# Attention scores, and the first v projection, computed in four 64x64 quarters of the TensorE array

## The chip, the cores and the metric

The kernel runs on one core of a Trainium2 chip. A core has a matrix engine (TensorE, PE in the profile, with its weight loads listed apart as PEld), a vector engine (VectorE, DVE), an activation engine (ScalarE, ACT), a general engine (GpSimd, POOL) and a queue that issues DMAs (SyncE, SP). TensorE writes its results to PSUM, eight banks of 512 fp32 columns on 128 partitions; the other engines work from SBUF or read PSUM. The metric is the device time of one execution in microseconds (us), smaller is better. Every time below comes from repeated runs of the kernel or from one execution taken by the hardware profiler.

## What is computed

The reference is one attention block on a picture of 48x48 = 2304 tokens with 512 channels, for 4 pictures:

```python
hn  = group_norm(x, 32 groups) * gn_scale + gn_bias
qkv = einsum('oc,bchw->bohw', qkv_w, hn) + qkv_b
q, k, v = qkv.reshape(b, 3, 8, 64, t).astype(float16)   # 8 heads of 64
w   = softmax(einsum('bhct,bhcs->bhts', q * scale, k * scale))
a   = einsum('bhts,bhcs->bhct', w, v).astype(float32)
out = x + einsum('oc,bchw->bohw', proj_w, a) + proj_b
```

Here b = 4, c = 512, t = 2304, and scale is 64 to the power of -1/4.

## The kernel before

**Tiling.** A batch's x lies in SBUF as 4 chunks of 128 channels by 5 token blocks (`QBLOCKS`: four of 512, one of 256). Heads are taken in pairs: a pair g (16 of them, 4 per batch) has one tile q and one tile k of 128 partitions, the even head in partitions 0 to 63 and the odd one in 64 to 127, by 2304 tokens, in fp16. The v values of two pairs lie in one tile with tokens on the partitions (18 tiles of 128 tokens, `NT`).

**Projections.** `qk_chain` (L709) makes a block of q or k: for each of 4 chunks, two fp32 matmuls with 64 weight columns each, one into PSUM partitions 0 to 63 and one into 64 to 127. `v_chain` (L760) makes v for two token tiles in one PSUM bank, again in two column halves: 2 tiles x 4 chunks x 2 halves = 16 matmuls of 256 columns; then one VectorE addition (L768) adds the bias and writes v. The trace shows each fp32 matmul as two records, one of each half starting together.

**Attention.** It runs over `stream`: for each pair and each query block a row of units, 27 per pair and so 432 in all. `scores` (L932) handles one unit: three PSUM tiles `ps` of two banks each. For each of them (a block of 512 queries) it multiplies 128 keys by 512 queries for both heads: two matmuls of 64 contraction rows and 128 weight columns, one per head, in the two row halves of the array, one per bank. In a block of 256 queries each `ps` tile takes two key tiles, so four matmuls of 256 columns. ScalarE then exponentiates the `ps` tile into p (L939). `values` (L957) multiplies p by v: 128 contraction rows, 64 weight columns per head, so two column halves. VectorE adds p over the units (L986); `add_up` (L1009) sums over the keys with a matmul against ones; `proj_chain` (L837) is the output projection, with the array undivided (128 weight columns, 128 rows).

**Order.** The program's order is written by hand. Before the attention (`alone` is true) the first pair's q and k and then batch 0's first v half are projected, with `ps` tiles as their banks (three `ps` tiles, two banks each). In the attention loop each step n issues the scores of unit n, VectorE's sum of unit n-1, pieces of projection work that a planner (`fill`) lets through against a credit, and the values of unit n-2. The planner's costs are constants in the code, so the order does not depend on measured time. TensorE works through its instructions in that order.

The lines that matter below: L709 (q and k projection), L760 and L768 (v projection and its evacuation), L932 and L939 (scores and exponential), L957 (values), L837 (output projection), L1009 (sums).

Of the kernel before, what the change touches and what calls it, by code (L numbers as in the profile page):

```python
# [12 lines left out]
F32 = mybir.dt.float32  # L13
F32R = mybir.dt.float32r
F16 = mybir.dt.float16
I32 = mybir.dt.int32
AF = mybir.ActivationFunctionType
ALU = mybir.AluOpType
# [4 lines left out]
B, C, T = 4, 512, 48 * 48  # L23
HEADS, D = 8, 64
GROUP = C // 32
EPS = 1e-5
P = 128
NC = C // P
NPAIR = HEADS // 2
NG = B * NPAIR  # L30
NT = T // P
# [11 lines left out]
QB = 512  # L43
# [424 lines left out]
def fast_path(  # L468
# [12 lines left out]
    nc = tc.nc  # L481
# [5 lines left out]
    vpool = ctx.enter_context(tc.tile_pool(name="vpool", bufs=1))  # L487
    apool = ctx.enter_context(tc.tile_pool(name="apool", bufs=2 * NPAIR - 1))
    ppool = ctx.enter_context(tc.tile_pool(name="ppool", bufs=3))
    work = ctx.enter_context(tc.tile_pool(name="work", bufs=2))  # L490
    small = ctx.enter_context(tc.tile_pool(name="small", bufs=2))
    dram = ctx.enter_context(tc.tile_pool(name="dram", bufs=4, space=DRAM))
    ps_s = ctx.enter_context(tc.tile_pool(name="ps_s", bufs=3, space=PSUM))
# [4 lines left out]
    hn = {}  # L498
# [24 lines left out]
    wqkv = const.tile([P, NC, 3 * C], F32, name="wqkv")  # L523
# [21 lines left out]
    bv = const.tile([P, C], F32, name="bv")  # L545
# [38 lines left out]
    def chain_bank(name):  # L584
        if alone[0]:
            return ps_s.tile([P, 2, QB], F32, tag="ps", name=name)[:, 0, :]
        return ps_w.tile([P, QB], F32, tag="pw", name=name)
# [88 lines left out]
    def chain_pieces(us, one, steps):  # L676


        def run(chunks):
            for c in chunks:  # L680
                one(c)

        return [
            piece(us * len(chunks), lambda chunks=chunks: run(chunks), i == 0, last)
            for i, chunks in enumerate(steps)
            for last in (i == len(steps) - 1,)
        ]
# [53 lines left out]
    vv = {}  # L741

    def v_chain(b, half, i):

        cols = bass.ts(half, C // 2)
        pw = {}

        def one(a):
            if a == 0:
                if i == 0:  # L750
                    vv[b, half] = vpool.tile(
                        [P, NT, C // 2], F16, tag=f"v{half}", name=f"v{half}_{b}"
                    )
                pw[0] = chain_bank(f"pv_{b}_{half}_{i}").rearrange(
                    "p (a n) -> p a n", a=2
                )
            at = (i + a) * P % QB
            for c in range(NC):
                for lo in (0, D):
                    nc.tensor.matmul(  # L760
                        pw[0][lo : lo + D, a, :],
                        hn[b, c, i * P // QB][:, at + lo : at + lo + D],
                        wqkv[:, c, 2 * C + half * C // 2 :][:, : C // 2],
                        start=(c == 0),
                        stop=(c == NC - 1),
                    )
            if a == 1:
                nc.vector.tensor_tensor(  # L768
                    vv[b, half][:, i : i + 2, :],
                    pw[0],  # L770
                    bv[:, cols].unsqueeze(1).to_broadcast((P, 2, C // 2)),
                    ALU.add,
                )

        return chain_pieces(1.72, one, (range(1), range(1, 2)))

# [140 lines left out]
    def scores(u):  # L920
        g, j, k, _ = u
        o, n = QBLOCKS[j]
        per = QB // n
        qt, kt = qk[g]
        pt = ppool.tile([P, BURST, 2, QB], F16, tag="p", name=f"p_{g}_{j}_{k}")
        for r in range(BURST):
            ps = ps_s.tile([P, 2, QB], F32, tag="ps", name=f"ps_{g}_{j}_{k}_{r}")
            for a in range(per):
                i = (k * BURST + r) * per + a
                for h in range(2):  # L930
                    rows = slice(h * D, (h + 1) * D)
                    nc.tensor.matmul(  # L932
                        ps[:, h, a * n : (a + 1) * n],
                        kt[rows, bass.ts(i, P)],
                        qt[rows, o : o + n],
                        start=True,
                        stop=True,
                    )
            nc.scalar.activation(pt[:, r], ps, AF.Exp)  # L939
        pts[u] = pt  # L940

# [327 lines left out]
        for p in qk_chain(0, 0, j):  # L1269
            p[1]()  # L1270
    for i in range(0, NT, 2):
        for p in v_chain(0, 0, i):
            p[1]()
    alone[0] = False

    credit = [0.0]
# [55 lines left out]
    for n in range(end):  # L1332
# [4 lines left out]
        if summed:  # L1337
            rows(*summed, add_up(*summed))
        wanted(stream[n][0])
        scores(stream[n])  # L1340
        if n > 0:
            add(stream[n - 1])
# [26 lines left out]
    g, b, j = NG - 1, B - 1, NQ - 1  # L1369
    n = QBLOCKS[j][1]  # L1370
# [44 lines left out]
@with_exitstack  # L1415
def group_norm_attention(ctx: ExitStack, tc: tile.TileContext, *args):
    nc = tc.nc
    keep = ctx.enter_context(tc.tile_pool(name="keep", bufs=1))
    flag = keep.tile([1, 1], I32, name="flag")

    kinds = mybir.EngineType
    engines = {kinds.PE, kinds.DVE, kinds.Pool, kinds.SP, kinds.Activation}
    with tc.manual_schedule(engines=engines):
        fast_path(tc, flag, *args)
    fails = nc.values_load(
        flag[0:1, 0:1],
        min_val=0,
        max_val=1,
        skip_runtime_bounds_check_because="it is the result of a comparison",
    )  # L1430
    with tc.If(fails > 0):
        general_path(tc, *args)
# [37 lines left out]
```

## Time and profile before

| | |
|---|---|
| median of 10 runs | 1618.52 us (1617.94 to 1619.9) |
| profiled execution | 1618.12 us, of which the profile's span is 1616.4 us |
| TensorE matmul | 1583.7 us busy, 98% of the span, 11500 records |
| TensorE weight load | 696.5 us, 43% |
| ScalarE | 1282.8 us, 79% |
| VectorE | 1136.6 us, 70% |
| GpSimd | 296.2 us, 18% |
| granted TensorE clock | 0.997 |

The span is what the profiler recorded from the first to the last instruction; 1.7 us of the run lie around it. A group line of the profile gives the source line, the engine, the operation, the tiles (output <- inputs), for TensorE the size of the part of the array (contraction rows * weight columns), the shape (partitions x elements and type), the number of instructions, then busy time and mean length of one, then how long the engine was idle before them and what ended the idle time. Matmuls are pipelined: their recorded length is longer than the distance from one to the next, so the cost of a matmul in a stream is read from the starts, not from the mean length. A timeline line gives the start in us from the span's start, the time to the last end, the engine, the line, the shapes and how many equal instructions it merges.

### The profile page before, as it was taken

The page shows a single profiled execution, that of the slowest core. Times are in us where ns is not written, and L with a number is a line of the kernel's source. Part 1 is how long each engine was busy: PE and PEld are TensorE (multiplying, and loading weights), DVE is VectorE, ACT ScalarE, POOL GpSimd, SP SyncE. Part 2 cuts the span into 40 slices and gives each one's busy share as a digit, 9 for nine tenths or more (in the row PEclk, how much of TensorE's full clock was granted, in tenths as well). Part 3 has the DMA queues.
Part 4 walks back from the last instruction along what each step waited for, and adds up shares of the span by engine and source line. Part 5 has one row for each costly group of instructions (what it writes and reads, how often), then busy time and mean ns, then how long its engine had stood idle before and what let it go on. Part 6 is the DMA issues. An engine that isn't in the chain of part 4 may idle for free.

```text
span 1616.4 us, 28315 instructions
## 1 busy us (share of the span) xinstructions
PE 1583.7 (98%) x11500; PEld 696.5 (43%) x11500; DVE 1136.6 (70%) x1302; ACT 1282.8 (79%) x1398; POOL 296.2 (18%) x419
## 2 busy tenths in 40 slices
PE   6999999999999999999999999999999999999996
PEld 2533434443333534555333353455533334435544
DVE  6167668866666678986666667898667666766775
ACT  3077777888888888888888878887888888888894
POOL 1001102211121221212111121121211121211211
PEclk9999999999999999999999999999999999999998
DMA  7002020000000024511000002352100000016423
GB/s 220 3 14 67 11 67 20 18 14 11 14 18 14 15 63 125 156 45 30 15 8 18 14 12 66 101 159 66 31 14 12 14 18 15 15 24 194 118 66 127
DMA packets 94898, 82.11 MB, mean 51 GB/s; under 512 B 50852, under 2 KB 60964, under 8 KB 94756
## 3 DMA queue, kind: packets, MB, share of 16 engines
q1 hardware_dynamic: 92724, 78.35, 17.5%
q8 instruction: 92, 1.51, 0.4%
q10 hardware_dynamic: 1904, 1.84, 0.4%
q14 instruction: 50, 0.41, 0.1%
q0 software_dynamic: 128, 0.01, 0.0%
HBM read 60.70 MB, written 19.17 MB: 49 GB/s over the span
## 4 chain that ended last, share of the span: by engine, by line
PE 92%; ACT 3%; issue 1%; DMA 1%; DVE 1%; SPq 0%; POOL 0%; ACTq 0%; DVEq 0%; POOLq 0%
PE pqk L709 29%; PE ps L932 19%; PE av L957 19%; PE pv L760 16%; PE pr L837 7%; ACT p L939 2%; PE ps L709 1%; PE sl L1009 1%; ACT a L831 1%; DMA x<-x_dram 1%; DMA sums<-slx 0%; DMA row<-inv 0%; DVE acc L986 0%; PE rest L837 0%; DVE r L860 0%
## 5 line engine op out<-in xcount | busy, mean ns | idle before, releaser
L939 ACT ACTIVATE p<-ps 128x1024 f16<-128x1024 f32 x1296 | 1231.9, 1027 | 298.4 <-PE ps L932 298.0
L986 DVE TENSOR_TENSOR acc<-acc,p 128x3072 f16<-128x3072 f16 x270 | 484.4, 1794 | 76.8 <-ACT p L939 76.0
L709 PE MATMUL pqk<-x,wqkv 128*64 128x512 f32 (+1 forms) x2464 | 519.3, 551 | 0.0
L932 PE MATMUL ps<-q,k 64*128 64x512 f16 (+1 forms) x2880 | 359.6, 358 | 6.2 <-ACT p L939 5.3
L957 PE MATMUL av<-p,v 128*64 128x512 f16 (+1 forms) x2880 | 361.1, 364 | 0.4 <-DVE slx L1025 0.3
L760 PE MATMUL pv<-wqkv,x 128*64 128x256 f32 x2304 | 268.6, 380 | 0.0
L709 PEld LDWEIGHTS pqk<-x,wqkv 128*64 128x64 f32 x2464 | 168.9, 137 | 224.2 <-issue 166.8
L1047 POOL TENSOR_SCALAR in<-sums 128x8 f32<-128x8 f32 (+1 forms) x158 | 110.3, 698 | 780.2 <-DMA sums<-slx 773.8
L932 PEld LDWEIGHTS <-k 64*128 64x128 f16 x2880 | 107.3, 94 | 286.1 <-issue 238.2
L957 PEld LDWEIGHTS <-v 128*64 128x64 f16 x2880 | 132.0, 109 | 210.7 <-issue 166.6
L1073 POOL TENSOR_TENSOR att<-avx,ib 128x512 f16<-128x512 f32 (+1 forms) x78 | 120.8, 1549 | 466.4 <-DMA ib<-row 416.8
L760 PEld LDWEIGHTS pv<-wqkv,x 128*64 128x64 f32 x2304 | 160.2, 137 | 92.8 <-issue 4.5
L986 DVE TENSOR_TENSOR acc<-p,p 128x3072 f16<-128x3072 f16 x79 | 138.1, 1748 | 0.0
L837 PE MATMUL pr<-a,whi 128*128 128x512 f32 (+1 forms) x312 | 122.2, 399 | 4.4 <-DVE r L860 3.2
L837 PE MATMUL pr<-a,wlo 128*128 128x512 f32 (+1 forms) x312 | 114.3, 373 | 0.0
L989 DVE TENSOR_TENSOR acc<-acc 128x1024 f16<-128x1024 f16 x156 | 110.1, 706 | 5.3
L719 DVE TENSOR_SCALAR q<-pqk,bqkv 128x512 f16<-128x512 f32 (+1 forms) x79 | 54.9, 695 | 80.3 <-PE pqk L709 80.0
L768 DVE TENSOR_TENSOR v<-pv,bv 128x512 f16<-128x512 f32 x72 | 49.7, 690 | 81.0 <-PE pv L760 80.8
L719 DVE TENSOR_SCALAR k<-pqk,bqkv 128x512 f16<-128x512 f32 (+1 forms) x75 | 52.2, 695 | 77.4 <-PE pqk L709 77.4
L966 DVE COPY avx<-av 128x512 f32<-128x512 f32 (+1 forms) x79 | 50.6, 640 | 66.1 <-PE av L957 66.0
L864 DVE SCALAR_TENSOR_TENSOR r<-pr,bproj,r 128x512 f32<-128x512 f32 (+1 forms) x80 | 54.9, 694 | 43.1 <-PE pr L837 42.4
L837 PEld LDWEIGHTS pr<-a,whi 128*128 128x128 f32 x312 | 58.5, 187 | 41.6 <-issue 18.7
(62 smaller groups left out, 453.3 us busy)
## 6 DMA issues: line engine op xcount, KB each, us to landing
r<-x_dram SPq DMA_DIRECT2D x72, 256.0 KB, 3.2
out_dram<-r SPq DMA_DIRECT2D x69, 256.0 KB, 2.1
ib<-row SPq DMA_DIRECT2D x126, 128.0 KB, 3.1
x<-x_dram SPq DMA_DIRECT2D x62, 256.0 KB, 4.1
x<-x_dram SPq DMA_DIRECT2D x16, 128.0 KB, 4.8
sums<-slx SPq DMA_DIRECT2D x128, 2.0 KB, 2.1
ib<-row SPq DMA_DIRECT2D x30, 64.0 KB, 3.1
wqkv<-qkv_wT_dram SPq DMA_DIRECT2D x2, 768.0 KB, 6.9
```

What stands on the lines that cost most here:

```text
L709: nc.tensor.matmul(pw[0][lo : lo + D, :n], wqkv[:, c, w0 + lo : w0 + lo + D], hn[b, c, j], start=(c == 0), stop=(c == NC - 1),)
L719: nc.vector.tensor_scalar(qk[g][part][:, o : o + n], pw[0][:, :n], bqkv[:, col : col + 1], SCALE, ALU.add, ALU.mult,)
L760: nc.tensor.matmul(pw[0][lo : lo + D, a, :], hn[b, c, i * P // QB][:, at + lo : at + lo + D], wqkv[:, c, 2 * C + half * C // 2 :][:, : C / ...
L837: nc.tensor.matmul(ps[:, :n], w[:, c, bass.ts(m, P)], at32[b, j, c], start=(i == 0), stop=(i == len(steps) - 1),)
L864: nc.vector.scalar_tensor_tensor(xt[:, i], places[i], bias, xt[:, i], ALU.add, ALU.add)
L932: nc.tensor.matmul(ps[:, h, a * n : (a + 1) * n], kt[rows, bass.ts(i, P)], qt[rows, o : o + n], start=True, stop=True,)
L939: nc.scalar.activation(pt[:, r], ps, AF.Exp)
L957: nc.tensor.matmul(av[0][lo : lo + D, :n], vv[b, pr // 2][:, i, pr % 2 * P + lo : pr % 2 * P + lo + D], pt[:, r, h, a * n : (a + 1) * n], ...
L986: nc.vector.tensor_tensor(t, before, pt, ALU.add)
L989: nc.vector.tensor_tensor(t[:, 0], t[:, 0], t[:, r], ALU.add)
L1047: nc.gpsimd.tensor_scalar(t, sm, limit, None, op)
L1073: nc.gpsimd.tensor_tensor(atts[g][:, o : o + n], avx.pop((g, j))[:, :n], ibs.pop((g, j))[:, :n], ALU.mult,)
```

## The change

Scores are computed in quarters: each matmul of 64 rows and 128 columns becomes two of 64 rows and 64 columns, for the lower and the upper half of the 128 keys. The order within a `ps` tile is: lower keys of the even head, lower keys of the odd head, upper keys of the even head, upper keys of the odd head. Banks, tiles and the exponential stay.

The nine pairs of token tiles of batch 0's first v half, which are made ahead of the attention, come from a new function `v_quarters` in place of `v_chain`. It splits the 128 channels of a chunk into two row halves as well; the row halves r = 0 and 1 accumulate in the two banks of one `ps` tile, and VectorE joins them in two additions: the first bank plus the bias into a tile t of fp32, then the second bank plus t into v. The other seven v halves, and q and k, are computed as before.

```diff
+    def v_quarters(b, half, i):
+        cols = bass.ts(half, C // 2)
+        ...
+        pw = ps_s.tile([P, 2, QB], F32, tag="ps", name=f"pv_{b}_{half}_{i}")
+        pw = pw.rearrange("p r (a n) -> p r a n", a=2)
+        for a in range(2):
+            at = (i + a) * P % QB
+            for c in range(NC):
+                x_c = hn[b, c, i * P // QB]
+                for lo in (0, D):
+                    for r in range(2):
+                        rows = slice(r * D, (r + 1) * D)
+                        nc.tensor.matmul(
+                            pw[lo : lo + D, r, a, :],
+                            x_c[rows, at + lo : at + lo + D],
+                            wqkv[rows, c, 2 * C + half * C // 2 :][:, : C // 2],
+                            start=(c == 0),
+                            stop=(c == NC - 1),
+                        )
+        t = work.tile([P, 2, C // 2], F32, tag="rows", name=f"vt_{b}_{half}_{i}")
+        nc.vector.tensor_tensor(
+            t, pw[:, 0], bv[:, cols].unsqueeze(1).to_broadcast((P, 2, C // 2)), ALU.add
+        )
+        nc.vector.tensor_tensor(vv[b, half][:, i : i + 2, :], pw[:, 1], t, ALU.add)
...
-                for h in range(2):
-                    rows = slice(h * D, (h + 1) * D)
-                    nc.tensor.matmul(
-                        ps[:, h, a * n : (a + 1) * n],
-                        kt[rows, bass.ts(i, P)],
-                        qt[rows, o : o + n],
-                        start=True,
-                        stop=True,
-                    )
+                for lo in (0, D):
+                    for h in range(2):
+                        rows = slice(h * D, (h + 1) * D)
+                        nc.tensor.matmul(
+                            ps[lo : lo + D, h, a * n : (a + 1) * n],
+                            kt[rows, i * P + lo : i * P + lo + D],
+                            qt[rows, o : o + n],
+                            start=True,
+                            stop=True,
+                        )
...
     for i in range(0, NT, 2):
-        for p in v_chain(0, 0, i):
-            p[1]()
+        v_quarters(0, 0, i)
```

## The prediction

> **What bounds the kernel now.** I read three views in this order: the page, to see which engine sets the end; the groups, for instruction counts; and a timeline of a few us of the attention on TensorE alone, because the change touches only how matmuls follow one another. First the page.
>
> ```profile
> PE 1583.7 (98%) x11500; PEld 696.5 (43%) x11500; DVE 1136.6 (70%) x1302; ACT 1282.8 (79%) x1398; POOL 296.2 (18%) x419
> PE 92%; ACT 3%; issue 1%; DMA 1%; DVE 1%; SPq 0%; POOL 0%; ACTq 0%; DVEq 0%; POOLq 0%
> L939 ACT ACTIVATE p<-ps 128x1024 f16<-128x1024 f32 x1296 | 1231.9, 1027 | 298.4 <-PE ps L932 298.0
> L932 PE MATMUL ps<-q,k 64*128 64x512 f16 (+1 forms) x2880 | 359.6, 358 | 6.2 <-ACT p L939 5.3
> L957 PE MATMUL av<-p,v 128*64 128x512 f16 (+1 forms) x2880 | 361.1, 364 | 0.4 <-DVE slx L1025 0.3
> L760 PE MATMUL pv<-wqkv,x 128*64 128x256 f32 x2304 | 268.6, 380 | 0.0
> L932 PEld LDWEIGHTS <-k 64*128 64x128 f16 x2880 | 107.3, 94 | 286.1 <-issue 238.2
> L957 PEld LDWEIGHTS <-v 128*64 128x64 f16 x2880 | 132.0, 109 | 210.7 <-issue 166.6
> ```
>
> TensorE is busy 98% and is 92% of the chain that ended last. The scores wait 5.3 us in all for ScalarE, while ScalarE waits 298 us for scores. So a nanosecond added to TensorE's sequence is a nanosecond of the run, and one saved there is saved. Now the sequence itself, from the timeline.
>
> ```profile
> 91.97 1.88 PE L709 MATMUL pqk<-x,wqkv 128*64 128x512 f32 x8
> 93.79 0.82 PE L932 MATMUL ps<-q,k 64*128 64x512 f16 x6
> 94.54 0.84 PE L957 MATMUL av<-p,v 128*64 128x512 f16 x6
> 95.21 2.31 PE L709 MATMUL pqk<-x,wqkv 128*64 128x512 f32 x10
> ...
> 94.02 0.59 PE L932 MATMUL ps<-q,k 64*128 64x512 f16 x4
> 94.23 0.38 PE L932 MATMUL ps<-q,k 64*128 64x512 f16 x2
> ...
> 94.78 0.60 PE L957 MATMUL av<-p,v 128*64 128x512 f16 x4
> ```
>
> Two matmuls in two halves start together; a pair of 512 fp16 columns follows the last after 0.21 to 0.22 us, and the fp32 pairs of L709 after 0.43. A burst of scores is three pairs, so 0.65 us of streaming. From its start to that of the values pass 0.75 us: 0.10 more. The eight L709 records are four pairs, 1.72 us, but the scores start after 1.82: again 0.10 more. From values back to L709 pass 0.67, only 0.02 more. So TensorE loses about 0.1 us on entry to the scores and 0.1 on leaving them, and none between values and projections, which use the same division of the array (128*64). Small losses after the switch: the second pair of scores comes 0.23 after the first, not 0.21, and the second pair of values 0.24 after theirs. There the weights could not be loaded ahead.
>
> Does the loss come from the rows or the columns of the division? The end of the trace has both kinds alone:
>
> ```profile
> 1569.39 0.40 PE L837 MATMUL pr<-a,whi 128*128 128x512 f32 x1
> 1569.63 0.40 PE L837 MATMUL pr<-a,wlo 128*128 128x512 f32 x1
> 1569.95 0.41 PE L1009 MATMUL sl<-acc,ones 128*64 128x512 f16 x2
> 1584.62 0.39 PE L837 MATMUL pr<-a,whi 128*128 128x512 f32 x1
> 1584.85 0.40 PE L837 MATMUL pr<-a,wlo 128*128 128x512 f32 x1
> 1585.18 0.83 PE L932 MATMUL ps<-q,k 64*128 64x256 f16 x12
> ```
>
> L837 matmuls are 0.23 to 0.24 apart. From 128*128 to 128*64 (columns alone change) pass 0.32, from 128*128 to 64*128 (rows alone) 0.33. Either change costs 0.09 to 0.10 us.
>
> **What the Trainium skill says.** The page "TensorEngine Tiling (Array Packing)", section "Key Properties", says that changing the tiling mode, not just the tile, drains TensorE; the 0.1 us above agree. The same page, "Restrictions", says that column tiling turns off the fast weight load, which "TensorE: Matmul & The Clock Gate", section "Weight-path perf modes", describes for full 128-column weights that are not fp32. The trace agrees: the 128-column loads of L932 take 94 ns, the 64-column ones of L957 109. Its Part 3 says that matmuls in different tiles run together, with four row tiles measured at 3.07 times one. The trace shows two at a time, never four.
>
> **The change, part by part.**
>
> *Scores, streaming.* 2880 matmuls become 5760, each with half the columns of the array and the same 512 or 256 moving columns. If four run together as two do now, a `ps` tile still costs one slot of 0.216 us (or two of 0.109), and nothing changes. The array was already full with two halves, so there is no throughput to win. The moving data is read twice per row half, as L957 already does for all 128 partitions. I take 0. Bounds: nothing below, since every cell is used now; above, see the rivals.
>
> *Scores, switches.* 64*128 becomes 64*64; values and projections stay 128*64. The number of columns now agrees with theirs and the number of rows does not, and a change of rows alone costs its 0.1 us in the lines above. So both switches stay: 0. If they went, see the first rival.
>
> *Scores, weight load.* After the drain the first loads are exposed. Today that is 0.226 against 0.216 to the second pair, 0.01 us, with the 128-column load; with the 64-column load the values show 0.240, 0.024 us. The quarters use 64-column loads, so +0.014 us on each of 432 bursts: +6.0 us. That assumes that four loads run side by side as two do. Bounds: 0 if one of them stays hidden, and another 0.024 x 432 = +10 if the two row halves of one column half load one after the other.
>
> *Scores, issue.* Two loads and two matmuls of a group start within 2 to 5 ns; four and four will take some 6 ns longer until the last quarter starts, and the drain on leaving waits for the last: 432 x 0.006 = +2.6 us. Bounds 0 and +5.
>
> *v ahead of the attention.* These are 288 records in 144 pairs of 0.216: 31.0 us between 45.4 and 76.4, TensorE alone. In quarters 576 records in 144 groups of four: the same 31.0 if four run together. Entry from L709 now costs a switch (+0.1), but the scores after it follow in the same mode (-0.1): 0. VectorE gets 9 more additions of 0.69 us (row L768, 690 ns). In this stretch it is busy 6 of 31 us, so 8 of them are hidden; TensorE goes around three `ps` tiles and needs each again only after two others, 7 us later. The last is not hidden: today the third `ps` tile of the first burst waits 0.26 us for L768; with two additions in a row it waits 0.69 longer. ScalarE's queue has not filled then, and TensorE moves on only after it: +0.7. Bounds 0.3 and 0.8.
>
> *Sum.* 6.0 + 2.6 + 0.7 = +9.3 us. On the profiled execution's own time, 1618.12, that is 1627.4; its run is 0.4 below the median of the runs, so about 1628 as a median. The mechanism's own range, from the bounds: +0.3 to +22, 1619 to 1640. What hides nothing here: no other engine gets shorter, ScalarE and VectorE have 20% and 30% of room, and no DMA is added.
>
> **The rivals.**
>
> *The switches go (faster).* If TensorE drains only when the number of columns changes, or if quarters and column halves count as one mode, then each burst saves 0.10 on entry, 0.10 in its own 0.75, and 0.02 after: 0.22 x 432 = 95 us at most; bursts next to L837 keep theirs, so about 85. ScalarE needs 3 x 1.027 = 3.08 us per burst and the attention has 1494/432 = 3.46 for one, so it lets most of that through. Time: about 1533. It decides as soon as over a tenth of the switches vanish. For it: columns would agree. Against: row changes alone cost 0.09 to 0.10.
>
> *Four do not run together (much slower).* If quarters go two by two, a burst costs 0.65 more: 432 x 0.648 = +280, and v +31: about 1929. With the skill's 3.07 in place of 4 it is 0.648 x 0.30 x 432 = +84, and with the rest about 1712. For it: the trace never shows four. Against: row halves (L932) and column halves (L957) each lose nothing.
>
> *Instruction supply.* The densest stream in the trace is L957 with 256 columns: two loads and two matmuls in 0.11 us. Quarters of 256 columns need twice that. If the rate is the limit, 48 bursts x 6 groups x 0.11 = +32: with the rest about 1659. Bursts of 512 columns need just the rate that is shown.
>
> *Nothing measurable.* Loads and issue stay hidden, only the 0.7 remains: 1619.
>
> That the change doesn't do what it says can be left out: the loops issue 64x64 pieces, and the array division is part of each instruction.
>
> **How the numbers follow.** What this measurement tells from no change is about 0.2%, 3.2 us. Forecast (slower by 3 to 22 us): 0.63. Four do not run together: 0.08. Supply: 0.06. Switches go: 0.08. Nothing measurable: 0.15, of which 0.01 may fall on the faster side. So faster 0.09, same 0.14, slower 0.77. The range takes the forecast, most of "nothing" and the supply case: 1616 to 1660, some 0.82 in all.
>
> **What the changed profile would show.** L709 to scores still 1.82, a burst 0.76 to 0.78 instead of 0.75, its second group 0.24 after the first, later ones 0.216 (0.109 at 256 columns); load length 109 ns; v ahead still 31 us with 18 additions; the third `ps` tile of the first burst waiting about 1 us for VectorE. I am wrong if a burst's start follows L709's last pair after 0.43 (switch gone), or if groups of four lie more than 0.22 apart.

## The result, and the profile after

The changed kernel takes 1625.63 us (median of 8 runs, 1625.03 to 1628.15) against 1618.43 of the kernel before (28 runs). The ratio is 1.0045, 95% interval 1.0037 to 1.0054: it is slower by 7.2 us. The profiled execution has a span of 1624.2 us, 7.8 more than the 1616.4 of before, at a granted TensorE clock of 0.998 against 0.997, so the clock is not the cause.

The page of the changed kernel, in the rows that answer to those shown of before (line, engine, operation, part of the array, shapes, count | busy us, mean ns of one | idle before, and what ended it):

```profile
PE 1591.4 (98%) x14668; PEld 721.1 (44%) x14668; DVE 1143.2 (70%) x1311; ACT 1282.9 (79%) x1398; POOL 298.9 (18%) x419
L971 ACT ACTIVATE p<-ps 128x1024 f16<-128x1024 f32 x1296 | 1232.0, 1026 | 306.1 <-PE ps L964 304.4
L964 PE MATMUL ps<-q,k 64*64 64x512 f16 (+1 forms) x5760 | 368.6, 362 | 6.4 <-ACT p L971 5.8
L989 PE MATMUL av<-p,v 128*64 128x512 f16 (+1 forms) x2880 | 361.0, 364 | 0.3 <-DVE slx L1057 0.3
L964 PEld LDWEIGHTS <-k 64*64 64x64 f16 x5760 | 130.5, 105 | 276.4 <-issue 237.8
```

L964 is now the line of the scores, L971 the exponential, L989 the values; L794 is v ahead of the attention, with its additions in L802 and L805. The matmuls of the scores have doubled from 2880 to 5760, and their busy time, in which overlapping records count once, grew only by 9.0 us: four run in the time of two. ScalarE's busy time is the same, and it waits 6.4 us longer for scores (304.4 against 298.0). So the added time is to be looked for in TensorE's sequence. The timeline of TensorE shows where it lies, in the same four steps as before (start, time to the last end, line, shapes, how many):

```profile
92.59 1.88 PE L709 MATMUL pqk<-x,wqkv 128*64 128x512 f32 x8
94.41 0.84 PE L964 MATMUL ps<-q,k 64*64 64x512 f16 x12
95.18 0.84 PE L989 MATMUL av<-p,v 128*64 128x512 f16 x6
95.85 0.60 PE L709 MATMUL pqk<-x,wqkv 128*64 128x512 f32 x2
...
94.65 0.60 PE L964 MATMUL ps<-q,k 64*64 64x512 f16 x8
94.86 0.39 PE L964 MATMUL ps<-q,k 64*64 64x512 f16 x4
```

From L709 to the scores pass 1.82 us, as before; the change of division still costs its 0.10. From values back to L709 pass 0.67, as before. The burst itself takes 0.77 from its start to that of the values, where it took 0.75. Within it the second group of four comes 0.24 after the first (0.23 before), the third 0.21 after the second, so only the first distance and the way out have grown. Read to the nanosecond from the records' starts, as medians over the bursts of 512 columns, with one more kernel that is told of below:

| ns, from start to start | before (two of 128 columns) | changed (four of 64) | eight of 32 |
|---|---|---|---|
| last pair of L709 to first scores | 528 | 526 | 526 |
| first scores to second group | 226 | 240 | 226 |
| second to third group | 216 | 216 | 216 |
| last group to first values | 309 | 316 | 330 |
| first to last piece within a group | 3 | 10 | 24 |

Summed over the 432 bursts, the distance to the second group adds 5.7 us (94.6 to 100.4) and the way out 3.1 (129.2 to 132.3). The way in takes 1.1 off (162.9 to 161.8, without the first burst, which follows v). The 2 ns of the way in lie between the first weight load and the first matmul: after L709 the load starts at 524 ns in both kernels, and the matmul follows it by 4 ns before, where two loads mostly go ahead of it, and by 2 ns in the changed kernel, where one does.

The longer distance to a second group belongs to the change of division: the second group of values comes after 240 ns where scores or L837 stand before it, and after 216 where L709 or L760 do, which use the division of the values. The scores show the same: in the changed kernel the first burst, which follows v in the same division 64*64, has its second group after 215 ns, and of the other 383 bursts of 512 columns 377 have it after 240 and six, which wait, later. That this is the time of a weight load that could not start early is the reading of the lines, not a separate test.

The start of the attention, in the timeline of TensorE of the kernel before:

```profile
45.21 31.25 PE L760 MATMUL pv<-wqkv,x 128*64 128x256 f32 x288
76.39 0.60 PE L932 MATMUL ps<-q,k 64*128 64x512 f16 x4
77.25 0.39 PE L932 MATMUL ps<-q,k 64*128 64x512 f16 x2 [0.26 <-DVE v L768]
77.58 0.65 PE L709 MATMUL pqk<-x,wqkv 128*64 128x512 f32 x2
```

and of the changed kernel:

```profile
45.13 31.31 PE L794 MATMUL pv<-wqkv,x 64*64 64x256 f32 x576
76.27 0.61 PE L964 MATMUL ps<-q,k 64*64 64x512 f16 x8
77.78 0.41 PE L964 MATMUL ps<-q,k 64*64 64x512 f16 x4 [0.90 <-ACT p L971]
78.12 0.65 PE L709 MATMUL pqk<-x,wqkv 128*64 128x512 f32 x2
```

The v stage ahead of the attention takes 31.1 us from its start to that of the scores with 576 records, against 31.2 with 288: no gain and no loss. From the start of v to the first L709 of the attention pass 32.99 us against 32.37: +0.62. The wait of the third `ps` tile is 0.64 longer, 0.90 instead of 0.26. The switch in front of the scores has moved to the front of v: from the last L709 group to v pass 313 ns instead of 216, and from the last v group to the scores 216 instead of 315, because both now use 64*64. With that entry v ahead costs +0.7 in all.

The parts sum to 5.7 + 3.1 - 1.1 + 0.7 = 8.4 us; the spans differ by 7.8 and the medians by 7.2. The records of the two traces can be matched group by group, which places the rest of the spans' difference: a wait of the output projection at 1044.6 us is 0.4 shorter, the third tiles of later bursts wait 0.2 less in all, and what is left cancels to within 0.1.

### The profile page after: what moved, and what is told of

Its sections match the earlier page's. It is cut to its first block, busy times and chain, and to the rows that moved or that the text cites. A ratio compares the mean times of both kernels' runs of the same rounds, so it can differ in the third digit from the quotient of the medians.

```text
span 1624.2 us, 34666 instructions
## 1 busy us (share of the span) xinstructions
PE 1591.4 (98%) x14668; PEld 721.1 (44%) x14668; DVE 1143.2 (70%) x1311; ACT 1282.9 (79%) x1398; POOL 298.9 (18%) x419
## 4 chain that ended last, share of the span: by engine, by line
PE 92%; ACT 4%; DMA 1%; issue 1%; DVE 1%; POOL 0%; SPq 0%; ACTq 0%; DVEq 0%; POOLq 0%
PE pqk L709 29%; PE ps L964 19%; PE av L989 19%; PE pv L760 14%; PE pr L867 7%; ACT p L971 3%; PE pv L794 2%; PE ps L709 1%; PE sl L1041 1%; ACT a L861 1%; DMA x<-x_dram 1%; DMA sums<-slx 0%; DVE r L890 0%; DMA row<-inv 0%; DVE acc L1018 0%
## 5 line engine op out<-in xcount | busy, mean ns | idle before, releaser
L971 ACT ACTIVATE p<-ps 128x1024 f16<-128x1024 f32 x1296 | 1232.0, 1026 | 306.1 <-PE ps L964 304.4
L709 PE MATMUL pqk<-x,wqkv 128*64 128x512 f32 (+1 forms) x2464 | 519.3, 551 | 0.0
L964 PE MATMUL ps<-q,k 64*64 64x512 f16 (+1 forms) x5760 | 368.6, 362 | 6.4 <-ACT p L971 5.8
L989 PE MATMUL av<-p,v 128*64 128x512 f16 (+1 forms) x2880 | 361.0, 364 | 0.3 <-DVE slx L1057 0.3
L709 PEld LDWEIGHTS pqk<-x,wqkv 128*64 128x64 f32 x2464 | 168.9, 137 | 223.6 <-issue 166.6
L1079 POOL TENSOR_SCALAR in<-sums 128x8 f32<-128x8 f32 (+1 forms) x158 | 114.4, 724 | 779.1 <-DMA sums<-slx 772.8
L964 PEld LDWEIGHTS <-k 64*64 64x64 f16 x5760 | 130.5, 105 | 276.4 <-issue 237.8
L760 PE MATMUL pv<-wqkv,x 128*64 128x256 f32 x2016 | 237.4, 380 | 0.0
L989 PEld LDWEIGHTS <-v 128*64 128x64 f16 x2880 | 131.9, 109 | 206.4 <-issue 162.2
L760 PEld LDWEIGHTS pv<-wqkv,x 128*64 128x64 f32 x2016 | 140.0, 137 | 81.6 <-issue 4.3
L768 DVE TENSOR_TENSOR v<-pv,bv 128x512 f16<-128x512 f32 x63 | 43.5, 691 | 56.1 <-PE pv L760 56.0
```

The lines of the kernel that those rows point to most:

```text
L709: nc.tensor.matmul(pw[0][lo : lo + D, :n], wqkv[:, c, w0 + lo : w0 + lo + D], hn[b, c, j], start=(c == 0), stop=(c == NC - 1),)
L760: nc.tensor.matmul(pw[0][lo : lo + D, a, :], hn[b, c, i * P // QB][:, at + lo : at + lo + D], wqkv[:, c, 2 * C + half * C // 2 :][:, : C / ...
L964: nc.tensor.matmul(ps[lo : lo + D, h, a * n : (a + 1) * n], kt[rows, i * P + lo : i * P + lo + D], qt[rows, o : o + n], start=True, stop=True,
L989: nc.tensor.matmul(av[0][lo : lo + D, :n], vv[b, pr // 2][:, i, pr % 2 * P + lo : pr % 2 * P + lo + D], pt[:, r, h, a * n : (a + 1) * n], ...
L1079: nc.gpsimd.tensor_scalar(t, sm, limit, None, op)
```

## The experiments

**Scores alone, v alone.** The change has two edits, so each was made without the other. The scores in quarters with v left as it was:

```diff
     for i in range(0, NT, 2):
-        v_quarters(0, 0, i)
+        for p in v_chain(0, 0, i):
+            p[1]()
```

> Scores in quarters as in the change, v ahead of the attention in halves as before. Theory (the cost is at the switches of every burst: 64-column loads exposed after the drain, and a last quarter that starts later): nearly all of the 7 us stay, +6.5 to +8 us against before (ratio about 1.0043), second group of a burst 0.240 after the first, values 0.316 after the last group. Rival (the two additions and the entry to v cost most of it): under +2 us.

Measured: 1627.13 us against 1618.34, ratio 1.0052 (1.0038 to 1.0065), second group at 240 ns, values at 316 ns. The 8.8 us are a little above the range that was expected. In the trace the scores' own terms are those of the change (5.8 and 3.1 us added, 1.0 taken off); another 1.1 us lies at about 16 us in the first pairs of L709, of which three follow after 0.85 us instead of 0.43, as some also do in the run of v alone. The reverse, with the scores loop as before:

```diff
...
-                for lo in (0, D):
-                    for h in range(2):
-                        rows = slice(h * D, (h + 1) * D)
-                        nc.tensor.matmul(
-                            ps[lo : lo + D, h, a * n : (a + 1) * n],
-                            kt[rows, i * P + lo : i * P + lo + D],
...
+                for h in range(2):
+                    rows = slice(h * D, (h + 1) * D)
+                    nc.tensor.matmul(
+                        ps[:, h, a * n : (a + 1) * n],
+                        kt[rows, bass.ts(i, P)],
...
```

> v ahead in quarters as in the change, scores in halves as before. Theory: one more switch on entry to v (+0.1), the late release of the last bank (+0.5): +0.6 us, not to be told from no change; v ahead itself takes 31.0 us with 576 matmul records. Rival (v in quarters costs most of the 7 us): +5 us or more.

Measured: 1618.97 us against the same 1618.34, ratio 1.0004 (0.9996 to 1.0013): no change that can be told. Its timeline on TensorE (here L962 is the scores and L969 the exponential):

```profile
46.48 31.31 PE L794 MATMUL pv<-wqkv,x 64*64 64x256 f32 x576
77.72 0.61 PE L962 MATMUL ps<-q,k 64*128 64x512 f16 x4
79.23 0.39 PE L962 MATMUL ps<-q,k 64*128 64x512 f16 x2 [0.90 <-ACT p L969]
```

The v stage alone makes the third scores tile wait 0.90 us, with the scores divided as before. The slowdown belongs to the scores. The two runs also show what a switch costs, at the one place where only the divisions differ: from the last v group to the first scores pass 315 ns before (128*64 to 64*128), 313 with the scores alone changed (128*64 to 64*64, rows only), 329 with v alone changed (64*64 to 64*128, columns only), and 216 with both changed (no switch).

**The order of the four.** If loads of one row half or of one column half wait for one another, the order matters.

```diff
-                for lo in (0, D):
-                    for h in range(2):
+                for h in range(2):
+                    for lo in (0, D):
```

> The change with the order of the four quarters of a tile turned: both key halves of the even head, then both of the odd head. If four loads run side by side whatever their order, the same as the change (+7 us against before, second group 0.240 after the first). If loads of one row half or of one column half wait for one another, the second group comes at 0.265 or later, and the run is about 10 us slower than the change, or faster if the order of the change was the bad one.

Measured: 1626.62 us, ratio 1.0047 (1.0032 to 1.0062), second group at 240 ns. The same as the change: the order makes no difference. In both kernels the four loads of a burst's first group start within 10 ns (median), and one takes 103 ns, so they run side by side.

**Eight pieces.** This separates the two terms, since one falls and the other grows with the number of pieces, and it doubles the rate of instructions.

```diff
-                for lo in (0, D):
+                for lo in range(0, P, 32):
...
-                            ps[lo : lo + D, h, a * n : (a + 1) * n],
-                            kt[rows, i * P + lo : i * P + lo + D],
+                            ps[lo : lo + 32, h, a * n : (a + 1) * n],
+                            kt[rows, i * P + lo : i * P + lo + 32],
```

> Scores in eight pieces of 64 rows and 32 columns, the rest as in the change. Theory of two terms: the exposed load halves with the columns (second group 0.229 after the first, -0.011 against quarters), the last of eight pieces starts about 0.013 later than the last of four (values 0.329 after the last group), so within 2 us of the change. Rival (rate of instructions): groups of 256 columns, with sixteen instructions for 0.109 us, stretch to 0.2 us or so: +25 us or more, all of it in the 48 bursts of the 256-query blocks.

Measured: 1627.56 us, ratio 1.0055 (1.0039 to 1.0070), within 2 us of the change. The timeline of TensorE in this kernel:

```profile
93.56 1.88 PE L709 MATMUL pqk<-x,wqkv 128*64 128x512 f32 x8
95.37 0.84 PE L964 MATMUL ps<-q,k 64*32 64x512 f16 x24
96.14 0.84 PE L989 MATMUL av<-p,v 128*64 128x512 f16 x6
...
1594.84 0.85 PE L964 MATMUL ps<-q,k 64*32 64x256 f16 x48
```

A burst takes 0.77, like one of quarters, but made up otherwise, as the table above shows: the second group is back at 226 ns, the way out has grown to 330. Take from each way out the time from the first to the last piece of a group: 309 - 3, 316 - 10, 330 - 24 are all 306 ns. So what follows waits for the start of the last piece plus a fixed time. In bursts of 256 columns the same subtraction gives 199 or 200 ns in all three kernels. The last line is a burst of 256 columns: 48 matmuls and 48 loads in 0.85 us, as long as the changed kernel takes with 24 of each:

```profile
1592.87 0.85 PE L964 MATMUL ps<-q,k 64*64 64x256 f16 x24
```

The rate of instructions is no limit here.

**What a switch costs in all.** Here the scores are put into the same division as values and projections, 128 rows and 64 columns, over both heads at once.

```diff
                 for h in range(2):
-                    rows = slice(h * D, (h + 1) * D)
-                    nc.tensor.matmul(
-                        ps[:, h, a * n : (a + 1) * n],
-                        kt[rows, bass.ts(i, P)],
-                        qt[rows, o : o + n],
...
+                    for lo in (0, D):
+                        nc.tensor.matmul(
+                            ps[lo : lo + D, h, a * n : (a + 1) * n],
+                            kt[:, i * P + lo : i * P + lo + D],
+                            qt[:, o : o + n],
...
```

> The kernel before with its scores in the division of the values (128 rows, 64 columns): four matmuls per tile, each over all 128 rows. The scores then mix the two heads of a pair, which leaves the separation of the heads out; the number of exponentials and all else stays. Streaming doubles, 0.648 us more per burst, +280 us in all. If a change of division is what costs 0.1 us on entry and 0.1 on leaving, both go, and with them the exposed loads, some 0.235 x 432 = 101 us: about 1797 us, projections to scores 1.72 us for four pairs. Rival (the loss belongs to the scores themselves, such as their wait for a free tile or a change of PSUM banks): it stays, and the run takes about 1898 us.

Measured in one execution of each: 1794.26 us beside 1618.85 of the kernel before, +175.4. The timeline of TensorE:

```profile
94.48 1.91 PE L709 MATMUL pqk<-x,wqkv 128*64 128x512 f32 x8
96.19 1.49 PE L932 MATMUL ps<-q,k 128*64 128x512 f16 x12
97.49 0.84 PE L957 MATMUL av<-p,v 128*64 128x512 f16 x6
98.14 3.63 PE L709 MATMUL pqk<-x,wqkv 128*64 128x512 f32 x16
```

From L709 to the scores pass 1.71 us, the bare four pairs (4 x 0.43), and from scores to values 1.30, the bare six (6 x 0.216). Nothing is lost on entry or exit, and 280 - 175 = 105 us went. By the starts of the records some 96 of them are switches and the loads exposed by them: 38.3 us on the ways in, 40.1 on the ways out, 17.4 before second groups. Most of the rest is another effect of the longer bursts: the scores waited 5.3 us for ScalarE before, and 0.3 here. So about 96 us is what the change could have won if it had removed the switches; apart from the one between v ahead and the scores, which moved to the front of v, it removed none.

**The third tile.** The last of the nine pieces of v ahead made in halves:

```diff
-        v_quarters(0, 0, i)
+        if i < NT - 2:
+            v_quarters(0, 0, i)
+        else:
+            for p in v_chain(0, 0, i):
+                p[1]()
```

> The change, but the last of the nine pairs of token tiles ahead of the attention is made in halves, with its one addition. If the 0.9 us that the third scores tile waits in the changed kernel comes from the tile it is given (that of the first scores tile, so that it waits for ScalarE's first exponential), the wait falls back to 0.2 to 0.3 us for VectorE, and the first projection piece after the burst starts about 0.5 us earlier against the start of the scores. If the second addition itself is what is waited for, the same. If neither, 0.9 us stay. The run as a whole within 1 us of the change.

Measured in one execution: 1627.06 us, 1.4 above the median of the change, which is more than the 1 us expected, but within its runs (1625.03 to 1628.15). In its timeline:

```profile
76.43 0.63 PE L964 MATMUL ps<-q,k 64*64 64x512 f16 x8
77.29 0.41 PE L964 MATMUL ps<-q,k 64*64 64x512 f16 x4 [0.24 <-DVE v L768]
77.63 1.94 PE L709 MATMUL pqk<-x,wqkv 128*64 128x512 f32 x8
```

The wait is back at 0.24, for VectorE. L709 follows 1.20 us after the start of the scores, where it followed after 1.85 in the changed kernel. By itself this does not choose between the second addition and the tile that is given. The trace of the changed kernel does, in the lines of ScalarE and VectorE:

```profile
76.70 2.85 ACT L971 ACTIVATE p<-ps 128x1024 f16<-128x1024 f32 x3 [46.06 <-PE ps L964]
77.24 0.69 DVE L805 TENSOR_TENSOR v<-pv,vt 128x512 f16<-128x512 f32 x1
```

The first exponential takes 1.02 us and ends at 77.73; the third scores tile starts at 77.78, before the second addition (L805) ends at 77.93. The programs as built agree: in the changed kernel the third scores tile lies in the banks of the first one, here in those of the last v piece.

The kernel with eight pieces shows the other case with the same two additions. There the third tile lies in the banks of the last v piece, and it waits for the second addition:

```profile
78.72 0.41 PE L964 MATMUL ps<-q,k 64*32 64x512 f16 x8 [0.98 <-DVE v L805]
```

## Why the prediction was right

It forecast 1628 us, slower, by one mechanism; 1625.6 was measured, +7.2 where +9.3 was summed. By its steps:

- *Scores, streaming, at 0.* Right. Four quarters follow one another at 216 ns (109 at 256 columns), as two halves do, and even groups of eight pieces do.
- *Scores, switches, at 0.* Right, and the first rival falls: the entry is 526 ns against 528, though the columns now agree with what comes before. It was worth what the rival said: some 96 us by the run in one division, against 95 at most.
- *Weight load, +6.0.* Measured +5.7. The exposed 64-column load cost the scores 24 ns as it does the values. That four loads run together, which the sum assumed, their starts show. A load of the scores takes 105 ns on average, where 109 was forecast from the values.
- *Issue, +2.6.* Measured +3.1: the last quarter starts 7 ns later, and the way out is 7 ns longer.
- *The way in* was taken as unchanged; it is 2 ns shorter, -1.1 us in all, between the first load and the first matmul.
- *v ahead, +0.7.* +0.7 measured; the stage is 31 us as forecast, and one switch moved from the scores to v (+0.1 and -0.1), as forecast. But the mechanism was not the one named. The prediction had the third scores tile wait for two VectorE additions in a row. In the changed kernel that tile gets the banks of the first scores tile, and it is ScalarE's first exponential that it waits for. The size was right by chance: 0.90 us for the one, and 0.98 for the other where, in eight pieces, the wait is the one that was named.
- *Rivals of throughput and supply.* The first falls with groups of four at 216 ns, the second with the 0.85 us for 24, and even for 48, matmuls in 256-column bursts.

The forecast sum lies 2.1 us above the medians' difference. The way in is 1.1 of that. About 0.6 are shorter waits elsewhere, and 0.6 is how far the two profiled executions lie further apart than the medians; the two terms of the scores, 0.3 below and 0.5 above their forecasts, nearly cancel.

## What to carry to other kernels

Where two halves already fill the array and each runs at its full rate, cutting them finer gains nothing, as here; what it changes is the edges of a burst, so the price here is the number of bursts times some 20 ns. A stream that alternates between divisions of the array pays about 0.1 us at each change, of rows as of columns; with the loads exposed after it, that is some 96 us of this kernel. That can be saved only by giving both sides the same rows and the same columns, or by changing less often, and here the same division would have doubled the scores' streaming.

## What was not expected

- Eight pieces of 64x32 in one slot: in bursts of 256 columns eight loads and eight matmuls go by in 0.109 us, one instruction in 7 ns, with no loss.
- The exposed load is not simply shorter with fewer columns: the second group comes after 226 ns with 128 columns, 240 with 64 and 226 with 32. The Trainium skill's page "TensorEngine Tiling (Array Packing)", section "Restrictions", names column tiling as what disables the fast weight load. The trace agrees for 128 against 64 columns (loads of 94 and 105 ns on average), and the 32-column load is short again (91 ns). Why is open.
- A later user of a PSUM tile can be given other banks, and with them another engine to wait for, without any edit at that place: the third scores tile waits 0.26 us for VectorE before, 0.90 for ScalarE in the changed kernel, and 0.98 for VectorE with eight pieces. The added VectorE instruction alone doesn't decide it, since the last two have the same v stage; what does is not shown.
